# Moving the last weight's split, the opening fold and the fetches of rows in a two-layer graph network kernel

## The chip, the cores and the metric

The kernel runs on one core of a Trainium2 chip. The metric is the device time of one execution in microseconds (us); lower is better. Times shown are medians of several runs. A profile is one further execution under the hardware profiler; its times are those of that execution alone.

## The reference

A batch of 32 graphs, each with 512 nodes and 512 features, goes through two layers. Both share one 512 x 512 adjacency matrix of zeros and ones.

```python
def _L0_gnn_ref(x, adj, Wq, bq, Wk, bk, Wv, bv):        # 8 heads of 64
    q = (x @ Wq + bq).reshape(b, n, H, HD)
    k = (x @ Wk + bk).reshape(b, n, H, HD)
    v = (x @ Wv + bv).reshape(b, n, H, HD)
    scores = jnp.einsum('bihd,bjhd->bhij', q, k) / jnp.sqrt(jnp.float32(HD))
    mask = jnp.where(adj == 0, jnp.float32(-1000000000.0), jnp.float32(0.0))
    weights = jax.nn.softmax(scores + mask[None, None, :, :], axis=-1)
    return jnp.einsum('bhij,bjhd->bihd', weights, v).reshape(b, n, H * HD)

def _L1_gnn_ref(x, adj, weight, bias):
    y = jnp.einsum('nm,bmd->bnd', adj, x)
    return jnp.einsum('bnd,do->bno', y, weight) + bias

x = _layernorm(x + _L0_gnn_ref(x, adj, ...), axis=-1)
x = _layernorm(x + _L1_gnn_ref(x, adj, ...), axis=-1)
```

## The kernel before, in words

All work on one graph ("batch" b) fits on the chip. A product that needs full float32 precision is made from three passes over numbers split in two: HIGH (a rounded part), REST (the remainder) and BOTH (a correction). ScalarE makes HIGH, VectorE or GpSimd makes REST and BOTH. The passes accumulate in PSUM banks, of which there are eight, handed out in a ring by `bank` (L200). A bank can be written again only once its reader has emptied it.

The order of the work is written out by hand. Each engine runs its instructions in the order in which the Python code issues them, and SyncE (SP) issues nearly all transfers, in order too: a transfer that must wait holds back those behind it. Python lists of small steps are interleaved by `merge` (L786): unit k, then the steps of slot k behind it. `run` (L719) issues them.

`iteration(b)` (L796) is one round of the loop, for b = 0 to 30; `last_halves` and the code behind it finish the last graph. A round works on several graphs at once, a software pipeline:

- `attend(b, hp)` (L619) multiplies the exponentials of head pair hp by the values, into one bank; `turn_out` (L629) has VectorE transpose that bank (L637) into `attT` and SP write it to memory (`turned`, L639). `fetch_rows` (L641) reads it back with four transfers in row order (L645).
- `take_scores(b, 1)` makes the scores of the second four heads on TensorE (L602). VectorE adds the mask and empties the banks into `e` (L604), ScalarE takes exponentials (L606), GpSimd adds them over the key blocks into `es` (L617). There are two score stages in a round: the second half of batch b and, later, the first half of batch b + 1.
- `projections(b + 1)` makes queries and keys in eight units of 12 matmuls each (L417): q0, k0, q1, k1 in the first half of the round, the other four in the second. A unit's weight, split in three, is a `chunk` of 768 KB that is streamed from memory for every batch: `fetch_chunk` (L406, its transfer is L412) writes into a ring of three buffers, and `project` (L431) fetches chunk n + 3 right behind its matmuls, into the buffer that these just left. ScalarE (L428) and VectorE (L429) add bias and parts. In the first half only chunk k1 is fetched and used within the half; q2, k2 and q3 are used in the second half.
- `fold_squares` (L647) sums exponentials on VectorE (transposes L655, sums L657), `pass_parts` and `fetch_parts` (L661, L666) send these sums through memory to turn them, `add_up` (L673) inverts them (L677, L678). `scale_rows` (ScalarE, L691) and `add_rows` (GpSimd, L695) make the residual.
- `values` are 48 matmuls; `aggregate` and `convolve` are the second layer of batch b - 1. `turns` and `splits_of_x` prepare batch b + 2: VectorE transposes (L347), ScalarE makes HIGH (L304), VectorE REST (L307), GpSimd BOTH (L310). `AFTER` (L868) holds steps that a round leaves for the next one, run after the first head pair of attention (`sooner`) and after the scores (`later`).
- In rounds 2 to 5, `load_adjacency_rows` (L288) loads 128 rows of the adjacency (256 KB), and `look_for_low_half` (L292) looks whether rounding would lose something of them.

Before the loop, the opening (L900 to L952) makes batch 0's projections and values, splits the weights, and keeps the chunks in memory for the later batches. The weight of the second layer, `w1`, is loaded by `load_last_weight` (L747, transfers L750) in four pieces while batch 0's values are made. `split_last_weight` (L755) then does three activations (L757, L758, L760) and two GpSimd subtractions (L761, L762) for each piece, just before the loop. `w1` is first used by `convolve` at the end of round 1.

Tiles come from rings of buffers by tag. `xs` has two, and holds in turn the last chunk of the opening, the adjacency, and then the batches' rows, loaded by `load(b)` (L215). `turn` has six and serves many short-lived tiles.

Of the kernel before, what the change touches and what calls it, by code (L numbers as in the profile page):

```python
# [8 lines left out]
FP = mybir.dt.float32  # L9
FR = mybir.dt.float32r  # L10
I32 = mybir.dt.int32
U8 = mybir.dt.uint8
AF = mybir.ActivationFunctionType
# [5 lines left out]
P = 128  # L19
# [4 lines left out]
EPSILON = 2.0 ** -12  # L24
SHRINK = 1.0 - 2.0 ** -13
SQ = 32
TURNS = 6
# [151 lines left out]
HIGH, REST, BOTH = 0, 1, 2  # L179
# [3 lines left out]
def fast_kernel(ctx: ExitStack, tc, verdict, x, adj, Wq, bq, Wk, bk, Wv, bv, W1, b1, out):  # L183
    nc = tc.nc
    B, N, D = x.shape
    H = Wq.shape[1] // HD
    HP = H // 2
    NB = N // P
    DB = D // P
# [4 lines left out]
    work = ctx.enter_context(tc.tile_pool(name="work", bufs=2))  # L194
# [5 lines left out]
    def bank(*shape):  # L200

        return psum.tile([P, *shape], FP, name="bank", tag="bank", bufs=8)

    def plain(t):

        return t.bitcast(FP)
# [3 lines left out]
    def rows_tile(b):  # L210
        if b == B - 1:
            return work.tile([P, NB, D], FP, name="xlast", tag="wv", bufs=1)
        return work.tile([P, NB, D], FP, name="xs", bufs=2)

    def load(b):  # L215
        X[b] = rows_tile(b)
        nc.sync.dma_start(X[b], x[b].rearrange("(c p) d -> p c d", p=P))
# [16 lines left out]
    RAW = {}  # L234
# [53 lines left out]
    def load_adjacency_rows(c):  # L288
        IN["adj", c] = work.tile([P, N], FP, name="adj_rows", tag="turn", bufs=TURNS)
        nc.sync.dma_start(IN["adj", c], adj[c * P:(c + 1) * P, :])  # L290
# [10 lines left out]
    PAIRS = GROUP // 2  # L301
# [60 lines left out]
    def turns(b):  # L362
        return [(turn_squares, b, d) for d in range(DB)] if b < B else []

    def splits_of_x(b):
        return [[(f, b, d) for d in range(DB)] if b < B else [] for f in (high_of_x, rest_of_x, both_of_x)]
# [95 lines left out]
    def projections(b):  # L462

        return [(project, b, which, m) for which, m in SEQUENCE] if b < B else []
# [120 lines left out]
    def aggregation(b):  # L585

        return [[(f, b, d) for d in range(DB)] if b >= 0 else [] for f in (split, aggregate)]
# [31 lines left out]
    def attend(b, hp):  # L619
        po = bank(N)  # L620
        for j in range(NB):
            e = E.pop((b, hp, j))
            for s in range(2):
                h = 2 * hp + s
                nc.tensor.matmul(po[s * HD:(s + 1) * HD, :], V[b, j][:, h * HD:(h + 1) * HD], e[:, s, :],  # L625
                                 start=(j == 0), stop=(j == NB - 1))
        OUT[b, hp] = po

    def turn_out(b, hp):  # L629

        po = OUT.pop((b, hp))
        at = AT[b, hp] = work.tile([P, N], FP, name="attT")
        if b == B - 1:
            nc.scalar.activation(at, po, AF.Copy)
            return

        nc.vector.transpose(at, po)  # L637
        TURNED[b, hp] = passing.tile([P, N], FP, name="turned")
        nc.sync.dma_start(TURNED[b, hp], at)  # L639

    def fetch_rows(b, hp):  # L641
        rows = ROWS[b, hp] = work.tile([P, NB, P], FP, name="rows")
        turned = TURNED.pop((b, hp)).rearrange("(i r) (c j f) -> j r c i f", r=SQ, c=NB, f=SQ)
        for j in range(P // SQ):
            nc.sync.dma_start(rows[j * SQ:(j + 1) * SQ, :, :].rearrange("p c (i f) -> p c i f", f=SQ), turned[j])  # L645
# [73 lines left out]
    def run(units):  # L719
        for unit in units:  # L720
            unit[0](*unit[1:])
# [23 lines left out]
    both_of_chunk(1)  # L745

    def load_last_weight():  # L747
        for d in range(DB):
            RAW["w1", d] = work.tile([P, D], FP, name="raw", tag="qk"[d % 2] + "0", bufs=PAIRS)
            nc.sync.dma_start(RAW["w1", d], W1[d * P:(d + 1) * P, :])  # L750

    def values_weight(d):
        return RAW["v", d // 2][:, d % 2, :]

    def split_last_weight(d):  # L755
        w = RAW.pop(("w1", d))
        nc.scalar.activation(w, w, AF.Copy, scale=1.0 / EPSILON)  # L757
        nc.scalar.activation(w1[:, HIGH, d, :], w, AF.Copy, scale=SHRINK)  # L758
        temp = work.tile([P, N], FR, name="temp", tag="turn", bufs=TURNS)
        nc.scalar.activation(temp, w, AF.Copy, scale=EPSILON * SHRINK)  # L760
        nc.gpsimd.tensor_sub(w1[:, REST, d, :], w, plain(w1[:, HIGH, d, :]))  # L761
        nc.gpsimd.tensor_sub(w1[:, BOTH, d, :], plain(w1[:, REST, d, :]), plain(temp))  # L762

    def norm(t, which):

# [6 lines left out]
    def folds(b, g):  # L772
        return [(fold_squares, b, hp) for hp in range(g * PAIRS, (g + 1) * PAIRS)]
# [5 lines left out]
    def residuals(b, g):  # L779

        return [[(f, b, hp) for hp in range(g * PAIRS, (g + 1) * PAIRS)] for f in (scale_rows, add_rows)]
# [4 lines left out]
    def merge(units, behind):  # L786

        merged = []
        for k in range(max(len(units), len(behind))):
            merged += units[k:k + 1] + (behind[k] if k < len(behind) else [])  # L790
        return merged
# [4 lines left out]
    def iteration(b):  # L796

        units = projections(b + 1)
        scaled, added = residuals(b, 0)
        later_scaled, later_added = residuals(b, 1)  # L800
        turned, divided = turns(b + 2), splits_of_x(b + 2)
        splits, gathered = aggregation(b - 1)
        squares = [(load_squares, b + 2, d) for d in range(DB)]
        folded = folds(b, 1)

        attend(b, 0)
        turn_out(b, 0)
        sooner, later = AFTER.pop(b - 1, ([], []))
        run(sooner)
        attend(b, 1)  # L810
        turn_out(b, 1)
        if b > 0:
            fetch_parts(b, 0)
        take_scores(b, 1)
        run(later)
        fetch_rows(b, 0)
        fetch_rows(b, 1)
        look = []
        if 2 <= b < 2 + NB:
            load_adjacency_rows(b - 2)  # L820
            look = [(look_for_low_half, b - 2)]
        if b == 0:
            run(merge(units[:4], [[(fold_squares, b, 1), (pass_parts, b, 0), (fetch_parts, b, 0)], [], [(add_up, b, 0)],
                                  folded[:1]]))
        else:
            old, young = norm(b - 1, 1), norm(b - 1, 0)
            roots = slice(0, 2 * NB if b > 1 else NB)
            if b == 1:
                run(survey(0, 0))
            run(merge(units[:4], [[(square_root, b - 1, roots), (add_up, b, 0), (invert_root, b - 1, roots)],  # L830
                                  folded[:1] + old[2:], [(store, b - 2)] if b > 1 else [], young[2:] + scaled]))
        attend(b, 2)
        turn_out(b, 2)
        load(b)
        attend(b, 3)
        turn_out(b, 3)
        if b == 0:
            run(scaled)
        later = scores(b + 1, 0)
        run(added + later + folded[1:])  # L840

        run(merge(units[4:], [[(pass_parts, b, 1), (fetch_parts, b, 1)], look, [(fold_squares, b + 1, 0)], splits[:2]]))
        units = values(b + 1)
        chunks = [(fetch_chunk, (b + 2) * len(SEQUENCE) + n) for n in range(AHEAD)]
        squares += [(fetch_rows, b, 2), (fetch_rows, b, 3), (pass_parts, b + 1, 0)] + chunks
        run(merge(units, [[(add_up, b, 1)], [(fold_squares, b + 1, 1)] + squares, later_scaled if b == B - 2 else [],
                          turned[:1] + (later_added if b == B - 2 else [])]))
        if b == B - 2:
            load(B - 1)
        run(merge(gathered, [[unit] for unit in turned[1:]]))  # L850
        fresh, seen, shift = survey(b, 0), survey(b - 1), biases(b - 1)
        high, rest, both = divided
        if b == 0:
            run(high + rest + both[::-1] + later_scaled + later_added)
            return
        convolve(b - 1, FIRST_TWO)
        if b == B - 2:
            run([(add_row, b - 1, 0), (add_row, b - 1, 1)] + shift[:2] + fresh + seen[:2])
            return
        run(later_scaled + later_added[:1] + [(add_row, b - 1, 0)] + shift[:1] + later_added[1:])  # L860
        run([(add_row, b - 1, 1)] + shift[1:2] + seen[:1])
        convolve(b - 1, whole(2))
        run([(add_row, b - 1, 2)] + shift[2:3] + fresh[:1])
        convolve(b - 1, whole(3))
        run(high + rest + [(add_row, b - 1, 3)] + shift[3:] + both)
        AFTER[b] = (fresh[1:] + seen[1:2], seen[2:])

    AFTER = {}  # L868
# [74 lines left out]
    w1 = work.tile([P, 3, DB, N], FR, name="w1", bufs=1)  # L943
# [2 lines left out]
    load_last_weight()  # L946
    run(merge(values(0), [[unit] for unit in turns(1)]))
    high, rest, both = splits_of_x(1)
    run(high + rest + both[::-1])

    fold_squares(0, 0)
    run([(split_last_weight, d) for d in range(DB)])  # L952
    for b in range(B - 1):
        iteration(b)
    last_halves(B - 1)
# [63 lines left out]
```

## Time and profile before

| what | value |
|---|---|
| median of 3 runs | 2574.64 us (2574.56 to 2575.02) |
| the profiled execution's own time | 2578.16 us |
| its span, from the first to the last instruction | 2575.9 us |
| mean granted clock of TensorE | 0.999 |
| transfers | 380.47 MB, mean 148 GB/s |
| busy: TensorE, VectorE, GpSimd, ScalarE | 99%, 80%, 68%, 59% |

How to read the profile: PE is TensorE, DVE VectorE, ACT ScalarE, POOL GpSimd, SP the queue that issues transfers. L417 is line 417 of the kernel before. A timeline line gives start, duration (us), engine, line, operation, what is written from what, how many instructions, and in brackets how long the engine was idle before and what ended the wait. A window line gives the stretch, its length, then for each engine the busy time and the number of instructions, the clock, the share of time that the DMA engines were busy and GB/s. Consecutive instructions of one kind are merged in a timeline, so pauses inside a merged line do not show. A matmul's end is modelled; lengths of TensorE's stages are read as differences of starts. Every landing of a transfer that the text gives is from the trace.

### The profile page before, as it was taken

The page shows a single profiled execution, that of the slowest core. Times are in us where ns is not written, and L with a number is a line of the kernel's source. Part 1 is how long each engine was busy: PE and PEld are TensorE (multiplying, and loading weights), DVE is VectorE, ACT ScalarE, POOL GpSimd, SP SyncE. Part 2 cuts the span into 40 slices and gives each one's busy share as a digit, 9 for nine tenths or more (in the row PEclk, how much of TensorE's full clock was granted, in tenths as well). Part 3 has the DMA queues.
Part 4 walks back from the last instruction along what each step waited for, and adds up shares of the span by engine and source line. Part 5 has one row for each costly group of instructions (what it writes and reads, how often), then busy time and mean ns, then how long its engine had stood idle before and what let it go on. Part 6 is the DMA issues. An engine that isn't in the chain of part 4 may idle for free.

```text
span 2575.9 us, 35702 instructions
## 1 busy us (share of the span) xinstructions
PE 2562.7 (99%) x11324; PEld 1693.9 (66%) x11324; DVE 2058.9 (80%) x3795; ACT 1527.3 (59%) x2540; POOL 1751.0 (68%) x1105
## 2 busy tenths in 40 slices
PE   9999999999999999999999999999999999999998
PEld 6566666766667666666667666676766667666666
DVE  8778788787787887878878778887788787887878
ACT  5666655657556665556665566655656556565555
POOL 5766676666766666766667667676766766666767
PEclk9999999999999999999999999999999999999999
DMA  9655554655545545456454464454654545545431
GB/s 267 165 158 142 159 146 125 174 140 162 148 112 167 152 151 162 110 154 176 135 160 119 143 178 136 153 138 129 172 141 161 143 117 167 145 157 164 103 124 52
DMA packets 675042, 380.47 MB, mean 148 GB/s; under 512 B 586912, under 2 KB 591264, under 8 KB 674848
## 3 DMA queue, kind: packets, MB, share of 16 engines
q1 hardware_dynamic: 674416, 377.48, 51.3%
q8 instruction: 92, 1.51, 0.2%
q14 instruction: 102, 0.84, 0.1%
q10 hardware_dynamic: 432, 0.66, 0.1%
HBM read 303.57 MB, written 74.45 MB: 147 GB/s over the span
## 4 chain that ended last, share of the span: by engine, by line
PE 94%; DVE 2%; DMA 1%; POOL 1%; ACT 1%; issue 0%; SPq 0%; DVEq 0%; ACTq 0%; POOLq 0%
PE bank L417 52%; PE bank L602 17%; PE bank L625 16%; PE bank L526 9%; DVE e L604 1%; DMA stream<-kept_k 0%; DMA turned<-attT 0%; DVE bnst L477 0%; DVE factors L307 0%; POOL es L617 0%; ACT e L606 0%; SPq L645 0%; POOL factors L310 0%; PE bank L729 0%; POOL wv L932 0%
## 5 line engine op out<-in xcount | busy, mean ns | idle before, releaser
L417 PE MATMUL bank<-factors,stream 128*128 128x512 f32 x3012 | 704.3, 392 | 2.9 <-DMA stream<-kept_k 2.3
L606 ACT ACTIVATE e<-e 128x1024 f32<-128x1024 f32 x512 | 525.3, 1055 | 300.7 <-DVE e L604 262.3
L417 PEld LDWEIGHTS bank<-factors,stream 128*128 128x128 f32 x3012 | 560.1, 188 | 167.7 <-DVE e L604 23.5
L617 POOL TENSOR_TENSOR es<-es,e 128x1024 f32<-128x1024 f32 x256 | 615.9, 2406 | 20.1
L604 DVE SCALAR_TENSOR_TENSOR e<-gap,bank 128x512 f32<-128x512 uint8 x1024 | 617.6, 678 | 12.1 <-PE bank L602 12.1
L617 POOL TENSOR_TENSOR es<-e 128x1024 f32<-128x1024 f32 x128 | 305.8, 2389 | 425.6 <-ACT e L606 425.6
L602 PE MATMUL bank<-q,k 64*128 64x512 f32 x2048 | 464.9, 598 | 0.7 <-DVE attT L637 0.7
L625 PE MATMUL bank<-e,v 128*64 128x512 f32 x2048 | 453.6, 595 | 0.0
L602 PEld LDWEIGHTS bank<-q,k 64*128 64x128 f32 x2048 | 204.1, 186 | 259.9 <-issue 157.3
L417 PE MATMUL bank<-w,factors 128*128 128x512 f32 x1536 | 354.4, 389 | 0.5 <-POOL factors L310 0.5
L417 PE MATMUL bank<-wv,factors 128*128 128x512 f32 x1536 | 353.5, 389 | 0.0
L310 POOL TENSOR_TENSOR factors<-factors,factors 128x512 fp32r<-128x512 f32 x255 | 322.1, 1284 | 33.9 <-DVE factors L307 32.0
L691 ACT ACTIVATE rows<-rows,zero,inverse 128x64 f32<-128x64 f32 x992 | 335.0, 429 | 9.7 <-DVE inverse L678 9.7
L417 PEld LDWEIGHTS bank<-w,factors 128*128 128x128 f32 x1536 | 288.0, 188 | 61.3 <-POOL factors L310 1.3
L417 PEld LDWEIGHTS bank<-wv,factors 128*128 128x128 f32 x1536 | 288.2, 188 | 60.6 <-DVE e L604 0.8
L625 PEld LDWEIGHTS bank<-e,v 128*64 128x64 f32 x2048 | 141.4, 137 | 278.4 <-issue 265.4
L503 ACT ACTIVATE high<-xs 128x512 fp32r<-128x512 f32 x124 | 74.4, 627 | 333.3 <-PE bank L526 333.2
L504 POOL TENSOR_TENSOR low<-xs,high 128x512 fp32r<-128x512 f32 x124 | 159.2, 1295 | 156.3 <-PE bank L526 156.3
L541 POOL TENSOR_TENSOR xs<-xs,b_r 128x512 f32<-128x512 f32 x124 | 159.8, 1289 | 125.3 <-DVE xs L561 125.3
L637 DVE STREAM_TRANSPOSE attT<-bank 128x512 f32<-128x512 f32 x124 | 87.6, 708 | 159.1 <-PE bank L625 159.1
L493 ACT ACTIVATE xs<-xs,shift,rstd 128x512 f32<-128x512 f32 x248 | 181.5, 805 | 14.7 <-DVE shift L488 14.7
L695 POOL TENSOR_TENSOR xs<-xs,rows 128x512 f32<-128x512 f32 x124 | 160.6, 1306 | 22.6 <-ACT rows L691 14.9
(98 smaller groups left out, 2433.4 us busy)
## 6 DMA issues: line engine op xcount, KB each, us to landing
stream<-kept_q SPq DMA_DIRECT2D x124, 768.0 KB, 5.9
stream<-kept_k SPq DMA_DIRECT2D x124, 768.0 KB, 4.3
xin<-in_x_dram SPq DMA_DIRECT2D x496, 64.0 KB, 2.3
turned<-attT SPq DMA_DIRECT2D x124, 256.0 KB, 3.2
rows<-turned SPq DMA_DIRECT2D x496, 64.0 KB, 2.4
xs<-in_x_dram SPq DMA_DIRECT2D x31, 1024.0 KB, 6.1
out_dram<-xs SPq DMA_DIRECT2D x31, 1024.0 KB, 5.1
part<-passed SPq DMA_DIRECT2D x256, 8.0 KB, 1.7
```

The lines of the kernel that those rows point to most:

```text
L310: engine.tensor_sub(both, plain(high), plain(rest))
L417: nc.tensor.matmul(pm, left(f, d), right(f, d), start=(f != REST and d == 0), stop=(f != HIGH and d == DB - 1))
L493: nc.scalar.activation(row, row, AF.Identity, bias=SHIFT[t][:, slot:slot + 1], scale=RSTD[t][:, slot:slot + 1])
L526: nc.tensor.matmul(pm, part, adjT[:, n % NB, :], start=(n == 0), stop=(n == 2 * NB - 1))
L541: nc.gpsimd.tensor_add(X[b][:, c, :], X[b][:, c, :], b1_r)
L602: nc.tensor.matmul(ps[s], keys[:, j * P:(j + 1) * P], queries, start=True, stop=True)
L604: nc.vector.scalar_tensor_tensor(e[:, s, :], gap[:, j, :], NEG * root, ps[s], op0=ALU.mult, op1=ALU.add)
L606: nc.scalar.activation(e, e, AF.Exp, scale=1.0 / root)
L617: nc.gpsimd.tensor_add(ES[b, hp], ES[b, hp] if j > 1 else E[b, hp, 0], E[b, hp, j])
L625: nc.tensor.matmul(po[s * HD:(s + 1) * HD, :], V[b, j][:, h * HD:(h + 1) * HD], e[:, s, :], start=(j == 0), stop=(j == NB - 1))
L691: nc.scalar.activation(part, part, AF.Identity, bias=zero, scale=inverse[:, c, s:s + 1])
L695: nc.gpsimd.tensor_add(cols, cols, ROWS.pop((b, hp)))
```

## The change

The change has three parts.

1. The last weight is loaded by one transfer into a tile of the `xs` ring. Its split moves out of the opening into round 0, behind the values of batch 1. It runs in two passes: first HIGH and REST of all four pieces, then ScalarE writes HIGH times EPSILON over the raw weight, and GpSimd subtracts this from REST. It has still twelve activations and eight subtractions; the four temporary tiles are gone.
2. In the opening, the remainders (REST) and corrections (BOTH) of batch 1's input are no longer issued ahead of `fold_squares(0, 0)` but left in `AFTER[-1]`, so that round 0 issues them after the first head pair's `attend` and `turn_out`.
3. In round 1, both `fetch_rows`, and in rounds 2 to 5 the second one, move from ahead of the projections to behind the first unit, that is, behind the fetch of chunk k1. In rounds 2 to 5 the adjacency rows are loaded behind `load(b)` instead of ahead of the projections. Round 0 and rounds from 6 on keep their order.

```diff
--- before.py
+++ after.py
@@ -745,21 +745,21 @@
     both_of_chunk(1)
 
     def load_last_weight():
-        for d in range(DB):
-            RAW["w1", d] = work.tile([P, D], FP, name="raw", tag="qk"[d % 2] + "0", bufs=PAIRS)
-            nc.sync.dma_start(RAW["w1", d], W1[d * P:(d + 1) * P, :])
+        RAW["w1"] = work.tile([P, DB, D], FP, name="xs", bufs=2)
+        nc.sync.dma_start(RAW["w1"], W1.rearrange("(c p) f -> p c f", p=P))
 
     def values_weight(d):
         return RAW["v", d // 2][:, d % 2, :]
 
-    def split_last_weight(d):
-        w = RAW.pop(("w1", d))
-        nc.scalar.activation(w, w, AF.Copy, scale=1.0 / EPSILON)
-        nc.scalar.activation(w1[:, HIGH, d, :], w, AF.Copy, scale=SHRINK)
-        temp = work.tile([P, N], FR, name="temp", tag="turn", bufs=TURNS)
-        nc.scalar.activation(temp, w, AF.Copy, scale=EPSILON * SHRINK)
-        nc.gpsimd.tensor_sub(w1[:, REST, d, :], w, plain(w1[:, HIGH, d, :]))
-        nc.gpsimd.tensor_sub(w1[:, BOTH, d, :], plain(w1[:, REST, d, :]), plain(temp))
+    def split_last_weight():
+        w = RAW["w1"]
+        for d in range(DB):
+            nc.scalar.activation(w[:, d, :], w[:, d, :], AF.Copy, scale=1.0 / EPSILON)
+            nc.scalar.activation(w1[:, HIGH, d, :], w[:, d, :], AF.Copy, scale=SHRINK)
+            nc.gpsimd.tensor_sub(w1[:, REST, d, :], w[:, d, :], plain(w1[:, HIGH, d, :]))
+        for d in range(DB):
+            nc.scalar.activation(w[:, d, :], plain(w1[:, HIGH, d, :]), AF.Copy, scale=EPSILON)
+            nc.gpsimd.tensor_sub(w1[:, BOTH, d, :], plain(w1[:, REST, d, :]), w[:, d, :])
 
     def norm(t, which):
 
@@ -813,12 +813,11 @@
             fetch_parts(b, 0)
         take_scores(b, 1)
         run(later)
-        fetch_rows(b, 0)
-        fetch_rows(b, 1)
-        look = []
-        if 2 <= b < 2 + NB:
-            load_adjacency_rows(b - 2)
-            look = [(look_for_low_half, b - 2)]
+        waiting = [(fetch_rows, b, 0), (fetch_rows, b, 1)]
+        looking = 2 <= b < 2 + NB
+        look = [(look_for_low_half, b - 2)] if looking else []
+        ready = 1 if looking else 0 if b == 1 else 2
+        run(waiting[:ready])
         if b == 0:
             run(merge(units[:4], [[(fold_squares, b, 1), (pass_parts, b, 0), (fetch_parts, b, 0)], [], [(add_up, b, 0)],
                                   folded[:1]]))
@@ -827,11 +826,14 @@
             roots = slice(0, 2 * NB if b > 1 else NB)
             if b == 1:
                 run(survey(0, 0))
-            run(merge(units[:4], [[(square_root, b - 1, roots), (add_up, b, 0), (invert_root, b - 1, roots)],
+            run(merge(units[:4], [waiting[ready:]
+                                  + [(square_root, b - 1, roots), (add_up, b, 0), (invert_root, b - 1, roots)],
                                   folded[:1] + old[2:], [(store, b - 2)] if b > 1 else [], young[2:] + scaled]))
         attend(b, 2)
         turn_out(b, 2)
         load(b)
+        if looking:
+            load_adjacency_rows(b - 2)
         attend(b, 3)
         turn_out(b, 3)
         if b == 0:
@@ -847,6 +849,8 @@
                           turned[:1] + (later_added if b == B - 2 else [])]))
         if b == B - 2:
             load(B - 1)
+        if b == 0:
+            split_last_weight()
         run(merge(gathered, [[unit] for unit in turned[1:]]))
         fresh, seen, shift = survey(b, 0), survey(b - 1), biases(b - 1)
         high, rest, both = divided
@@ -946,10 +950,9 @@
     load_last_weight()
     run(merge(values(0), [[unit] for unit in turns(1)]))
     high, rest, both = splits_of_x(1)
-    run(high + rest + both[::-1])
-
+    run(high)
     fold_squares(0, 0)
-    run([(split_last_weight, d) for d in range(DB)])
+    AFTER[-1] = (rest + both[::-1], [])
     for b in range(B - 1):
         iteration(b)
     last_halves(B - 1)
```

## The prediction, made before the change was run

> **What bounds the kernel now.** I read the page's busy times first. TensorE is busy for 99% of the span, so the ceiling on a change that leaves the matmuls alone is what TensorE loses to waits.
>
> ```profile
> PE 2562.7 (99%) x11324; PEld 1693.9 (66%) x11324; DVE 2058.9 (80%) x3795; ACT 1527.3 (59%) x2540; POOL 1751.0 (68%) x1105
> ```
>
> The busy share hides slow pacing, so next I cut the trace into one window per loop round. Each begins where a batch's first attention matmul begins (rounds 1 to 6, of which 2 to 5 carry the adjacency look).
>
> ```profile
> 115.17:196.74 81.57, 79.87 (x354) 52.55 (x353) 63.63 (x114) 51.63 (x95) 55.55 (x35) 1.00 0.58 165
> 196.74:276.62 79.88, 79.85 (x353) 52.53 (x353) 64.82 (x120) 47.86 (x82) 54.81 (x34) 1.00 0.53 150
> 276.62:357.07 80.45, 79.81 (x353) 52.54 (x352) 64.83 (x121) 47.88 (x82) 54.80 (x34) 1.00 0.53 149
> 357.07:436.69 79.62, 79.62 (x354) 52.62 (x353) 64.83 (x120) 47.88 (x82) 54.81 (x34) 1.00 0.52 151
> 436.69:517.05 80.36, 79.86 (x355) 52.54 (x354) 65.03 (x121) 47.88 (x82) 54.81 (x34) 1.00 0.53 149
> 517.05:596.66 79.61, 79.61 (x354) 52.62 (x354) 63.50 (x118) 47.34 (x81) 54.34 (x34) 1.00 0.51 148
> ```
>
> The second column is the length. An undisturbed round takes 79.61 us (the last one); rounds 1, 2, 3 and 5 are longer by 1.96, 0.27, 0.84 and 0.75 us. From here on the kernel repeats. So I read TensorE's timeline, first an undisturbed round (517 us on), then rounds 0 and 1.
>
> ```profile
> 524.06 7.21 PE L602 MATMUL bank<-q,k 64*128 64x512 f32 x32
> 531.20 11.21 PE L417 MATMUL bank<-factors,stream 128*128 128x512 f32 x48
> 542.34 7.09 PE L625 MATMUL bank<-e,v 128*64 128x512 f32 x32
> ```
>
> Differences of starts give stage lengths: scores (L602) 531.20 - 524.06 = 7.14 us, first half of the projections (L417) 542.34 - 531.20 = 11.14.
>
> ```profile
> 56.91 8.27 PE L602 MATMUL bank<-q,k 64*128 64x512 f32 x32
> 65.11 11.17 PE L417 MATMUL bank<-factors,stream 128*128 128x512 f32 x48
> ...
> 83.23 2.85 PE L602 MATMUL bank<-q,k 64*128 64x512 f32 x12
> 86.74 6.48 PE L602 MATMUL bank<-q,k 64*128 64x512 f32 x20 [0.66 <-DVE attT L637]
> 93.15 11.22 PE L417 MATMUL bank<-factors,stream 128*128 128x512 f32 x48
> ...
> 129.33 8.49 PE L417 MATMUL bank<-factors,stream 128*128 128x512 f32 x36
> 139.52 2.97 PE L417 MATMUL bank<-factors,stream 128*128 128x512 f32 x12 [1.70 <-DMA stream<-kept_k]
> ```
>
> Round 0's two score stages take 65.11 - 56.91 = 8.20 and 93.15 - 83.23 = 9.92 us, 1.06 and 2.78 over the reference. Only 0.66 of these 3.84 us shows as idle: the rest is TensorE pacing itself on banks that VectorE empties late. Round 1's projection half waits 1.70 us for a k chunk, the fourth of the half. Why VectorE is late in round 0 stands in the timelines of ScalarE and VectorE:
>
> ```profile
> 59.85 0.63 ACT L757 ACTIVATE raw<-raw 128x512 f32<-128x512 f32 x1 [7.88 <-DMA raw<-in_L_gnn_weight_dram]
> 66.68 7.68 ACT L606 ACTIVATE e<-e 128x1024 f32<-128x1024 f32 x8
> 74.27 0.66 ACT L428 ACTIVATE q<-bank,bq_c 128x512 f32<-128x512 f32 x1
> ```
> ```profile
> 74.96 0.69 DVE L429 TENSOR_TENSOR q<-bank,q 128x512 f32<-128x512 f32 x1 [6.17 <-ACT q L428]
> 82.60 0.27 DVE L677 TENSOR_REDUCE inverse<-part 128x16 f32<-128x64 f32 x1 [3.38 <-DMA part<-passed]
> ```
>
> ScalarE stands 7.88 us before the last weight, splits it until 66.78, and only then takes the exponentials; VectorE idles 6.17 us for the bias add behind them, then 3.38 us for the sums' round trip, and reaches the transposes of the attention output (L637) at 85.98, after TensorE wants their banks. And the late chunk of round 1, in the SP queue:
>
> ```profile
> 129.07 5.32 SPq L645 DMA_DIRECT2D rows<-turned  x8
> 134.48 0.57 SPq L412 DMA_DIRECT2D stream<-kept_k  x1
> ```
>
> The chunk's buffer is free about 129.33 + 2.75 = 132.1 (a quarter of the half), but eight row fetches stand ahead of it until 134.39.
>
> **What the Trainium skill says.** "DMA: Bandwidth & Descriptors", section "Anatomy of one DMA": a semaphore wait happens on the issuing sequencer, not in the DMA engines. The trace agrees: the chunk issues 0.09 us after the last row fetch. The same page, "Queues, rings and completion order": each DMA engine consumes one queue's descriptors in ring order. The trace agrees: the first head's turned tile, issued at 58.67, lands at 62.51, 0.68 after the last of the four weight loads (61.83). "SBUF — State Buffer", "Who interferes with whom": a VectorE operation with two SBUF inputs is blocked while GpSimd holds the shared port. The trace agrees: the first remainder (L307, 0.68 us otherwise) at 51.24 takes 2.60 us, over GpSimd's L617 that ends at 53.29.
>
> **Fold ahead of remainders (round 0's opening).** Now VectorE does four remainders (51.24 to 55.65), four fold operations (55.57 to 58.02), two L637 transposes, and starts the mask-and-add L604 at 59.18, 2.27 us after the scores start; in round 1 it is 123.35 - 122.19 = 1.16 us. Afterwards the fold runs at 51.24 to 53.7, the first L637 to 54.3 (its bank is ready near 49.90 + 3.70 = 53.6, the delay of the same step at 142.42), the remainders to 54.3 + 4 x 0.61 = 56.7 without GpSimd in the way, the second L637 at 56.91 + 0.13 = 57.04. L604 then starts at 58.07: **-1.06 us** on the path. GpSimd's four L310 (4.96 us) follow the remainders, 56.7 to 61.7; they are needed 1.84 us into the first projection, at 65.9. Cover lost, the wait would be what exceeds 4.2 us.
>
> **Last weight out of round 0's start.** Twelve activations and eight subtractions leave ScalarE and GpSimd between 59.85 and 71.73. Exponentials start near 59.5 and end near 68.9, the bias add comes 4.7 us after the projections start (as at 134.06 against 129.33), so near 69.6 instead of 74.96. Fold of head pair 1 to 72.5, its sums' round trip 4.55 us (78.05 to 82.60 now): add-up at 77.2, third fold near 78.4 to 80.8 (its GpSimd sums are ready by 69), L637 at 80.8 and at 82.9. TensorE then wants the first bank six banks, 2.85 us, into the stage. Slack: 1.4 us on VectorE. So the second stage is 7.14 too: **-2.78 us**. With VectorE's slack gone, each further us of round trip costs up to one, at most the 2.78 again.
>
> **Where the split goes.** Twelve activations x 0.62 = 7.4 us into an idle stretch of ScalarE (12.50 us ahead of 116.68) and eight GpSimd subtractions x 1.31 (pitch at 61.22 to 71.73) = 10.5 us into one of 12.29 us ahead of 120.89: cost **0**. ScalarE's second pass waits for GpSimd's remainders, some 6 us after its own start, still 2 us before the next splits. GpSimd's last subtractions can hold VectorE's first remainder for up to 0.9 us; the second L637 waits for TensorE anyway, with 0.94 us to spare. Uncovered, 0 to 0.6 us. The weight is first used near 185, far off. One load of 1 MB instead of four of 256 KB moves the same bytes: 0. It lies in an xs buffer that the next load needs only at 147.
>
> **A new wait in round 0.** Its rows still go ahead of the chunk (the order changes from round 1 on). Their start hangs on the turned tile behind the weight (62.51), not on VectorE, so the fourth chunk still lands at 72.64, the trace's landing now. TensorE wants it at 64.05 + 8.3 = 72.35 instead of 73.4: about 0.3 us, with the restart 0.5. Bounds 0 (landing 0.4 earlier) and 0.9. I take **+0.5**.
>
> **Rows behind the chunk, round 1.** The chunk issues near 132.4 and takes 3.8 to 4.9 us (undisturbed 3.97 at 534.28; 4.90 here), so lands by 137.3, needed at 137.6: 13.09 (142.42 - 129.33) becomes 11.14, **-1.95**. The eight rows issue 5.3 us long behind it and land near 140.5; ScalarE scales them at 145.03, so 4.5 us of cover.
>
> **Half of the rows and the adjacency rows behind the chunk, rounds 2 to 5.** SP is on time there (the chunk issues 3.05 to 3.09 after the half begins), but 64 KB rows and a 256 KB load lie ahead in the ring and landing takes 5.3, 5.9, 4.6 and 5.8 us; about 5.2 is allowed. Taking four rows and about 0.7 us of adjacency data out gives 4.3 to 4.9: **-(0.27 + 0.84 + 0 + 0.75) = -1.86**. The adjacency rows, now behind the batch load, land near 316 in round 3; the look uses them at 322.83. The later two-row fetches have the same cover as in round 1.
>
> **Sum.** -1.06 - 2.78 + 0.5 - 1.95 - 1.86 = -7.15 us. The profiled execution took 2578.16 us, span 2575.9; its span should become 2568.8. The median shown, 2574.64, lies 3.5 under that execution's time; waits are differences within the program, so I take the sum off it: **2567.5 us** (-0.28%).
>
> **Rivals.** (a) The sums' round trip takes the place of the weight: it comes earlier but behind other queue entries, and the second score stage stays long. VectorE's 3.38 us idle speaks for it, 1.4 us slack against. 2567.5 + 2.8 = 2570.3. (b) The chunks stay late since the DMA engines, not the order, are slow: landings of 5.9 us in round 3 against 4.6 in round 4 with the same queue speak for it. Rounds 1 to 5 keep 3.8 us: 2571.3. (c) The split is moved but nothing gained, because opening waits only shift: 2574.6. (d) **Slower**: row fetches behind the chunk land after ScalarE wants to scale; the exponentials of the next batch queue behind that, and TensorE with them, in rounds 1 to 5. Cover is 4.5 us; every us beyond costs 5 us in all. It decides once rows land 4.5 + 7.15 / 5 = 5.9 us later than reckoned; at 7 us, 2567.5 + 12.5 = 2580. Row landings of 2 to 3 us after issue speak against it.
>
> **How the numbers follow.** Forecast 0.66 (own range 2566.2 to 2569.2), (a) 0.13, (b) 0.12, (c) 0.04, (d) 0.05. What a measurement can tell from no change is about 0.2%, 5.15 us: faster is below 2569.5, so the forecast and a part of (a), 0.71; within, the rest of (a), (b), (c), 0.24; slower, (d), 0.05. The range, 2566.2 to 2571.5, takes in (a) and (b), the k chunk's bounds and 0.5 us more for the opening.
>
> **What would show it.** Right: both score stages of round 0 at 7.14, rounds 1 to 5 at 79.6, ScalarE's exponentials near 59.5, the split in the gap ahead of 113, a small wait for the fourth chunk of round 0. Wrong: L637 still the releaser in round 0, chunk waits in rounds 1 to 5, or new waits on GpSimd's L310 or on the scaled rows.

## The result, and the profile after

The changed kernel took 2569.23 us (median of 16 runs, 2568.46 to 2571.19), the kernel before beside it 2574.43 us (16 runs). The ratio is 0.998, 95% interval 0.9973 to 0.9987: 5.2 us faster, at the edge of the 0.2% named above. That is 0.03 us outside the forecast's own range (2566.2 to 2569.2) and inside the wider one, which takes in rivals (a) and (b). The profiled execution of the changed kernel took 2569.64 us, its span is 2567.9 us. A second set of runs of the same kernel gave a ratio of 0.9978 (0.9969 to 0.9987).

TensorE's share of busy time on the page has hardly anywhere left to go:

```profile
PE 2557.3 (100%) x11324; PEld 1692.1 (66%) x11324; DVE 2058.6 (80%) x3795; ACT 1528.6 (60%) x2540; POOL 1751.1 (68%) x1105
```

The windows of rounds 1 to 6, cut as before (stretch, length, busy time and count for TensorE, weight loads, VectorE, ScalarE, GpSimd, then clock, share of DMA, GB/s):

```profile
112.00:192.34 80.34, 79.82 (x353) 52.56 (x352) 63.82 (x114) 51.51 (x95) 58.99 (x38) 1.00 0.61 167
192.34:271.89 79.55, 79.55 (x354) 52.64 (x353) 64.81 (x120) 47.87 (x82) 54.81 (x34) 1.00 0.53 151
271.89:351.44 79.55, 79.55 (x354) 52.64 (x353) 64.82 (x120) 47.86 (x82) 54.83 (x34) 1.00 0.53 151
351.44:431.24 79.80, 79.80 (x354) 52.55 (x353) 64.81 (x119) 47.87 (x82) 54.84 (x34) 1.00 0.54 150
431.24:510.77 79.53, 79.53 (x354) 52.63 (x353) 65.05 (x121) 47.88 (x82) 54.86 (x34) 1.00 0.54 151
510.77:590.30 79.53, 79.53 (x353) 52.63 (x352) 63.52 (x118) 47.34 (x81) 54.35 (x34) 1.00 0.53 148
```

An undisturbed round is 79.53 us here and was 79.61 in the profile of before. No step of the change explains that: the same code runs at 79.53 in some sets of runs and at 79.60 in others, and the medians of the kernel before follow (2574.4 and 2574.3 with the one, 2576.7 and 2577.0 with the other). So a span is never compared below across sets; each round is measured against the undisturbed one of its own trace. By that, round 1 still loses 0.81 us and round 4 0.27. The two spans differ by 8.0 us, of which this change of pace is over 2.

TensorE's timeline of rounds 0 and 1:

```profile
57.19 7.21 PE L602 MATMUL bank<-q,k 64*128 64x512 f32 x32
64.33 8.45 PE L417 MATMUL bank<-factors,stream 128*128 128x512 f32 x36
72.93 3.00 PE L417 MATMUL bank<-factors,stream 128*128 128x512 f32 x12 [0.15 <-DVE part L657]
75.86 7.09 PE L625 MATMUL bank<-e,v 128*64 128x512 f32 x32
82.88 7.21 PE L602 MATMUL bank<-q,k 64*128 64x512 f32 x32
90.02 11.18 PE L417 MATMUL bank<-factors,stream 128*128 128x512 f32 x48
...
126.16 8.45 PE L417 MATMUL bank<-factors,stream 128*128 128x512 f32 x36
135.14 3.00 PE L417 MATMUL bank<-factors,stream 128*128 128x512 f32 x12 [0.52 <-DMA stream<-kept_k]
```

Both score stages of round 0 are 7.14 us (64.33 - 57.19 and 90.02 - 82.88), from 8.20 and 9.92. The fourth unit of the first projection half begins at 72.93 instead of 72.62 (64.33 + 8.29), the small new wait that was forecast; the half is 0.4 us longer than an undisturbed one (11.53 against 11.10). The line names VectorE, but chunk k1 landed at 72.80 and VectorE had nothing that this unit needs: it is the DMA. Round 1 still waits for its chunk. ScalarE and VectorE in round 0:

```profile
59.73 4.64 ACT L606 ACTIVATE e<-e 128x1024 f32<-128x1024 f32 x4 [7.47 <-DVE e L604]
64.82 4.33 ACT L606 ACTIVATE e<-e 128x1024 f32<-128x1024 f32 x4 [0.45 <-POOL es L617]
69.06 0.67 ACT L428 ACTIVATE q<-bank,bq_c 128x512 f32<-128x512 f32 x1
```
```profile
54.51 2.46 DVE L307 SCALAR_TENSOR_TENSOR factors<-factors,turn 128x512 fp32r<-128x512 f32 x4
...
69.77 0.69 DVE L429 TENSOR_TENSOR q<-bank,q 128x512 f32<-128x512 f32 x1 [1.76 <-ACT q L428]
...
79.16 0.26 DVE L677 TENSOR_REDUCE inverse<-part 128x16 f32<-128x64 f32 x1 [5.13 <-DMA part<-passed]
...
82.53 1.30 DVE L637 STREAM_TRANSPOSE attT<-bank 128x512 f32<-128x512 f32 x2
```

The exponentials start at 59.73 instead of 66.68, and the bias add no longer waits 6 us. The four remainders take 2.46 us instead of 4.41, since GpSimd no longer holds the first one up. The sums' round trip is now what VectorE waits for (5.13 us), and the transposes L637 end only 0.2 us before the masks need VectorE. The split's new place, on GpSimd:

```profile
105.39 5.07 POOL L759 TENSOR_TENSOR w<-xs,w 128x512 fp32r<-128x512 f32 x4
110.43 5.01 POOL L762 TENSOR_TENSOR w<-w,xs 128x512 fp32r<-128x512 f32 x4
117.94 4.97 POOL L310 TENSOR_TENSOR factors<-factors,factors 128x512 fp32r<-128x512 f32 x4 [2.50 <-DVE factors L307]
```

Its eight subtractions end at 115.44, 2.5 us before GpSimd's next work. They cost nothing on the path. The SP queue of round 1:

```profile
129.20 0.34 SPq L412 DMA_DIRECT2D stream<-kept_k  x1
129.65 6.56 SPq L645 DMA_DIRECT2D rows<-turned  x8
```

The chunk is issued 3.04 us into the half, as early as it can be, with nothing ahead of it. It landed 5.80 us later all the same (135.00).

### The profile page after: what moved, and what is told of

Read it like the earlier page. It is cut to its first block, busy times and chain, and to the rows that moved or that the text cites. A ratio compares the mean times of both kernels' runs of the same rounds, so it can differ in the third digit from the quotient of the medians.

```text
span 2567.9 us, 35669 instructions
## 1 busy us (share of the span) xinstructions
PE 2557.3 (100%) x11324; PEld 1692.1 (66%) x11324; DVE 2058.6 (80%) x3795; ACT 1528.6 (60%) x2540; POOL 1751.1 (68%) x1105
## 4 chain that ended last, share of the span: by engine, by line
PE 98%; DVE 1%; DMA 0%; issue 0%; POOL 0%; ACT 0%; DVEq 0%; ACTq 0%
PE bank L417 54%; PE bank L602 18%; PE bank L625 17%; PE bank L526 9%; DVE e L604 0%; DMA stream<-kept_k 0%; DVE bnst L477 0%; POOL factors L310 0%; DMA xin<-in_x_dram 0%; DVE early L316 0%; DVE factors L307 0%; DVE xlast L561 0%; DVE xs L557 0%; DVE xlast L557 0%; PE bank L701 0%
## 5 line engine op out<-in xcount | busy, mean ns | idle before, releaser
L310 POOL TENSOR_TENSOR factors<-factors,factors 128x512 fp32r<-128x512 f32 x255 | 321.9, 1282 | 25.4 <-DVE factors L307 24.7
L637 DVE STREAM_TRANSPOSE attT<-bank 128x512 f32<-128x512 f32 x124 | 87.8, 709 | 156.4 <-PE bank L625 156.4
```

The lines of the kernel that those rows point to most:

```text
L310: engine.tensor_sub(both, plain(high), plain(rest))
```

## The experiments

My theory after the result: the round 0 terms are right; in rounds 1 to 5 the saving was overestimated, since the first profile drew unusually late chunks and since rows behind a chunk hinder it too. The rival: order in the queue decides alone, as the forecast had it, and round 1's wait is an accident. In what follows, "excess" is a round's length over the undisturbed round of the same trace (79.60 us, a mean, in both profiles of the kernel before), and a landing is the time from the issue of chunk k1 to its landing.

**The kernel before, again.** No edit.

> The kernel before, unchanged, profiled once more. If the waits in its first profile are fixed by the program: rounds 1, 2, 3 and 5 are again 1.95, 0.27, 0.84 and 0.75 us over 79.6, and the score stages of round 0 take 8.20 and 9.92 us. If the chunk's landing is a matter of chance from one execution to the next, as the profiled execution's 2578.2 us against a median of 2574.4 suggests: round 0 as before, but another set of rounds late, by about 1 to 2 us in all instead of 3.8. Timed against itself: ratio 1.000.

Ratio 1.000 (0.9992 to 1.0009). In the new profile rounds 1 to 5 have an excess of 1.39, 0.32, 0.01, 0.69 and 0.01 us, 2.42 in all against 3.87 (1.97, 0.28, 0.85, 0.02, 0.75) in the first; round 0's second score stage is 8.95 against 9.92. Which rounds wait, and how long, changes from one execution to the next. So a sum of waits from one trace is one draw.

**Parts 1 and 2 alone; part 3 alone.** In the first kernel, the fetches of rows and adjacency are back where they were:

```diff
-        run(waiting[:ready])
+        fetch_rows(b, 0)
+        fetch_rows(b, 1)
+        if looking:
+            load_adjacency_rows(b - 2)
```

> The weight's split moved and the fold ahead, but rows and adjacency where they were. By the forecast's sum: -1.06 - 2.78 + 0.5 = -3.3 us against before, both score stages of round 0 at 7.14, rounds 1 to 5 as late as in before. If the chunk's lateness in the timed runs is worth only about 1.5 us, this kernel is nearly as fast as the changed one (within 1.5 us); if it is worth the 3.8 us of the first profile, it is 3.8 us slower than the changed one.

Ratio 0.9988 (0.9981 to 0.9995): -2.96 us (2573.76 against 2576.72). Round 0 goes to 61.75 us; the second score stage is 7.45, not 7.14. The second kernel is the kernel before with the third part of the change only.

> Only rows and adjacency moved behind the chunks; opening and split as before. By the forecast -3.8 us against before. If the first profile of before drew unusually late chunks, -1 to -2 us. Round 0 as before (8.20 and 9.92 us). If rows behind the chunk slow its landing, round 1 still waits some 0.5 us or more for chunk k1, landing near 5.8 us.

Ratio 0.9991 (0.9983 to 0.9999): -2.05 us. The interval reaches from -0.3 to -4.4 us, so the time alone doesn't exclude the forecast's -3.8; the profiles below tell more. Round 1's chunk lands after 5.62 us, rounds 1 to 5 have an excess of 1.26 in all. The two gains add up to 5.0 us, the whole change's 5.2: in this cut the parts are independent, as far as intervals of about 2 us either way can tell.

**Rows behind the chunk in every round.**

```diff
-        ready = 1 if looking else 0 if b == 1 else 2
+        ready = 0 if b > 0 else 2
```

> The changed kernel with both row fetches behind chunk k1 in every round from 1 on. If only what lies ahead of the chunk in the queue delays it (the forecast's reckoning): chunk landings of 4.0 to 4.5 us in all rounds and no change against the changed kernel. If rows that follow right behind it slow it: landings of 5.2 to 5.8 us in every round as in round 1 of the changed kernel, each round 0.3 to 0.8 us longer, 30 rounds, so 10 to 20 us slower than the changed kernel.

Ratio 0.9999 (0.999 to 1.0007): the whole gain is lost again. In rounds 6 to 29 the median landing is 5.00 us against 4.23 in the changed kernel, where rows go ahead; six of 24 landings exceed 5.2 us, none does there. Rounds 1 to 30 have an excess of 6.4 us. Round 10, in TensorE's timeline and in the SP queue of this kernel:

```profile
845.12 8.50 PE L417 MATMUL bank<-factors,stream 128*128 128x512 f32 x36
853.88 3.00 PE L417 MATMUL bank<-factors,stream 128*128 128x512 f32 x12 [0.27 <-DMA stream<-kept_k]
```
```profile
848.21 0.34 SPq L412 DMA_DIRECT2D stream<-kept_k  x1
848.65 6.29 SPq L645 DMA_DIRECT2D rows<-turned  x8
855.04 0.65 SPq L412 DMA_DIRECT2D stream<-kept_q  x1
```

The chunk landed 5.54 us after its issue, at 853.75. Not all of the excess is of this kind: 1.4 us of it stand in the second halves of rounds 5 and 27, where chunk k3 is late (6.0 and 5.4 us after its issue) with no rows behind it. There the transfers that stand behind the rows in the queue were later too, and the last of them landed 1.6 to 1.8 us after k3 was issued.

The loss is smaller than the 10 to 20 us expected, since most landings stay just within the 5.2 us allowed. But the direction is plain: rows that follow a chunk delay its landing. That the queue ran empty before the chunk is not the reason: chunk k3, issued 5 us after the last landing and followed by nothing for 3 us, lands in 4.19 us (median, rounds 6 to 28 of the changed kernel).

The trace's records of single DMA packets narrow the delay down. With rows behind it, the last of the chunk's 128 packets ends 4.01 us after the issue; for chunk k3 in the changed kernel it is 3.81 (medians of rounds 6 to 28). But the landing, the signal that TensorE waits for, comes 1.04 us after that last packet, against 0.39. So most of the delay is not in moving the chunk's data. It lies between the last packet and the signal, while the rows' packets of 128 bytes are under way (the first of them begins 3.4 us after the chunk's issue).

**Only the adjacency moved in rounds 2 to 5.**

```diff
-        ready = 1 if looking else 0 if b == 1 else 2
+        ready = 0 if b == 1 else 2
```

> The changed kernel, but in rounds 2 to 5 both row fetches go ahead of the chunk again; only the adjacency rows stay moved. If rows ahead of the chunk delay it (forecast): landings of about 4.8 us in rounds 2 to 5 or more, no gain or a loss up to 0.5 us against the changed kernel. If rows behind it slow it and the adjacency alone was the hindrance: landings of 4.0 to 4.5 us in rounds 2 to 5 as in later rounds, those rounds at 79.55, up to 0.5 us faster than the changed kernel.

Ratio 0.9977 (0.9968 to 0.9987). Landings in rounds 2 to 5 are 4.20, 4.75, 4.49 and 4.33 us, none of those rounds has an excess over 0.02. So the adjacency alone was the hindrance there, and the change's move of the second row fetch isn't needed. In time the kernel isn't told apart from the changed one (0.998 and 0.9978).

**Rows of round 1 behind the second unit.** In addition to the edit above, both fetches of round 1 stand behind chunk q2, and the second one of round 0 behind chunk k1.

```diff
-        ready = 0 if b == 1 else 2
+        ready = (1, 0)[b] if b < 2 else 2
...
-            [waiting[ready:] + [(square_root, ...), ...], folded[:1] + old[2:], ...
+            [[(square_root, ...), ...], waiting[ready:] + folded[:1] + old[2:], ...
```

> As the kernel with only the adjacency moved, and in round 1 both row fetches go behind the second unit's chunk fetch instead of the first's, in round 0 the second row fetch goes behind chunk k1. If rows right behind a chunk slow it: round 1's chunk lands in about 4.3 us instead of 5.8 and its wait of 0.5 us (0.8 us of stage length) goes; round 0's half is shorter by up to 0.4 us, unless rows slow that chunk as well. In all 0.8 to 1.5 us faster than the changed kernel. If they do not: round 1's chunk still lands after 5 us or more, no difference.

Ratio 0.9976 (0.9967 to 0.9986), no difference from the last kernel, so the gain that was expected did not come. Round 1's chunk lands in 4.38 us and the round is 79.61, but in the last kernel, with the rows right behind it, it landed in 5.03 us, which is also in time. Over eight executions with the rows right behind, round 1's landing was 4.70 to 5.80 us, late in two. Round 0 is 61.86 against 61.85.

**Part 1 alone.** The weight's split moved, the remainders ahead of the fold, rows and adjacency as before:

```diff
-    run(high)
+    run(high + rest + both[::-1])
     fold_squares(0, 0)
-    AFTER[-1] = (rest + both[::-1], [])
```

> The weight's split alone is moved, remainders stay ahead of the fold, rows and adjacency as before. By the forecast: first score stage of round 0 stays at 8.2, the second goes to 7.14: -2.78 us against before, less up to 0.5 for chunk k1. If the second stage needs the fold's earlier start as well, it stays above 7.14 and the gain is smaller.

Ratio 0.999 (0.9982 to 0.9999): -2.35 us. The score stages of round 0 are 8.18 and 7.40: as forecast, each stage has its own cause, though the second stays 0.26 us above 7.14.

**Part 2 alone.** The fold ahead of the remainders in the kernel before, with the split where it was:

```diff
-    run(high + rest + both[::-1])
+    run(high)
     fold_squares(0, 0)
+    AFTER[-1] = (rest + both[::-1], [])
     run([(split_last_weight, d) for d in range(DB)])
```

> The fold alone goes ahead of the remainders; the split stays in the opening. By the forecast: first score stage of round 0 at 7.14 (-1.06 us), the second stays near 9.9 since ScalarE still stands before the last weight: -1.06 us against before. A rival: the second stage grows by what the first one gains, as its late VectorE steps hang on the weight's landing and not on the scores, and nothing is gained.

Both expectations fell: ratio 1.004 (1.0026 to 1.0053), 9.1 us **slower**. TensorE's and GpSimd's timelines of this kernel:

```profile
57.28 7.21 PE L602 MATMUL bank<-q,k 64*128 64x512 f32 x32
64.42 2.14 PE L417 MATMUL bank<-factors,stream 128*128 128x512 f32 x8
76.20 11.93 PE L417 MATMUL bank<-factors,stream 128*128 128x512 f32 x40 [9.65 <-POOL factors L310]
```
```profile
60.86 1.28 POOL L761 TENSOR_TENSOR w<-raw,w 128x512 fp32r<-128x512 f32 x1 [7.22 <-DMA turned<-attT]
...
69.99 1.27 POOL L762 TENSOR_TENSOR w<-w,temp 128x512 fp32r<-128x512 f32 x1
71.22 4.94 POOL L310 TENSOR_TENSOR factors<-factors,factors 128x512 fp32r<-128x512 f32 x4
```

The first score stage is 7.14, as expected. But the corrections L310 moved along with the remainders, and on GpSimd they now stand behind the split's eight subtractions, which wait for the weight. They end at 76.16; the first projection wants them 1.9 us into its run. Without the first part, the second is a loss.

**The changed kernel, again.**

> The changed kernel, unchanged, on the same chip and beside the same runs of before as the three kernels that follow. If its profile is typical: rounds 2 to 5 with chunk landings of 4.7 to 5.3 us, round 1 between 4.8 and 5.8 us, 5 us faster than before (ratio 0.998), and up to 1 us slower than the kernel that moves only the adjacency in rounds 2 to 5. If round 1's wait in its first profile was chance, round 1 is near 79.6 here.

Ratio 0.9978 (0.9969 to 0.9987). Rounds 1 to 5 have an excess of 0.39 us in all, 0.30 of it in round 5 (landing 5.26); round 1 is in time (4.95 us). Round 0 is 61.52, its second score stage 7.25.

**Fold earlier in round 0**, on the kernel with only the adjacency moved:

```diff
         if b == 0:
+            fold_squares(b, 1)
-            run(merge(units[:4], [[(fold_squares, b, 1), (pass_parts, b, 0), ...
+            run(merge(units[:4], [[(pass_parts, b, 0), ...
```

> The kernel with only the adjacency moved in rounds 2 to 5, and in round 0 the fold of head pair 1 ahead of the first projection unit's bias add, in an idle stretch of VectorE (1.8 us). If the round trip of the sums now limits round 0's second score stage (7.55 us in that kernel, 7.14 undisturbed), it starts up to 1.8 us earlier and the stage goes to 7.14: 0.4 us less, round 0 at 61.45 instead of 61.85. If it is the fold behind the round trip, or the wait only moves to the fourth chunk, round 0 stays at 61.85.

Inconclusive: ratio 0.9979 (0.9971 to 0.9987). The second stage is 7.14, but in this execution chunk k1 came 1 us late (12.34 us for the half), which gives VectorE time anyway. Whether the earlier fold helps stays open.

**Adjacency load in rounds 2 to 29, ahead of the chunk and behind the batch's load.** Both kernels start from the one with only the adjacency moved, and repeat load and look in every round:

```diff
-        looking = 2 <= b < 2 + NB
+        looking = 2 <= b < B - 2
```

The first puts the load ahead of the units, the second leaves it behind `load(b)`.

> Load and look of adjacency rows in each of rounds 2 to 29 (they are repeated; the output is the same), the load ahead of chunk k1 where the kernel before had it, both row fetches ahead too. If 256 KB ahead of the chunk in the queue delay it (forecast): chunk landings of 4.6 to 5.9 us in every round and rounds 0.2 to 0.8 us longer, 8 to 20 us in all against the next kernel. If the late landings of rounds 2 to 5 came from elsewhere: landings of 4.0 to 4.5 us, no difference from the next kernel.

> The same load and look in each of rounds 2 to 29, but the load behind the batch's load, as the change puts it. Both theories: chunk landings of 4.0 to 4.5 us, rounds of 79.6, within 1 us of the kernel that moves only the adjacency in rounds 2 to 5. If the load there disturbs later transfers (batch load, chunk k3), rounds are longer by that.

Ahead: ratio 1.0004 (0.9995 to 1.0012), 2575.53 us. Behind: 0.9979 (0.997 to 0.9988), 2569.0 us. The 6.5 us between them are the price of 28 loads in the wrong place, less than the 8 to 20 us expected. The SP queue of round 12 with the load ahead, where the chunk landed 4.50 us after its issue:

```profile
998.86 5.32 SPq L645 DMA_DIRECT2D rows<-turned  x8
1004.22 0.62 SPq L290 DMA_DIRECT2D adj_rows<-in_adj_dram  x1
1005.51 0.34 SPq L412 DMA_DIRECT2D stream<-kept_k  x1
```

Landings in rounds 6 to 29:

| what stands around chunk k1 in the queue | kernel | median landing | least to most |
|---|---|---|---|
| rows ahead | changed | 4.23 us | 4.02 to 4.95 |
| rows ahead, adjacency load elsewhere in every round | loads behind | 4.16 us | 3.89 to 4.74 |
| rows and adjacency load ahead | loads ahead | 4.86 us | 4.25 to 5.63 |
| nothing ahead, rows right behind | rows behind | 5.00 us | 4.49 to 5.75 |

The second kernel's excess in rounds 2 to 29 is 0.3 us in all: the load does no harm where the change puts it.

## Why the prediction was right, and which term was too large

**First score stage of round 0, -1.06.** Right: 8.20 to 7.14, for the reason given, with the start of the masks 1.16 us after the stage's start. But the step hid a condition. "Cover lost, the wait would be what exceeds 4.2 us" named the price of late corrections, and no step asked what stood ahead of them on GpSimd. With the weight's split still there, it was 9.65 us.

**Second score stage, -2.78.** Nearly right: 9.92 to 7.14 in the first profile after, to between 7.14 and 7.55 in the others. The slack of 1.4 us was mis-sized. It took the sums' round trip at 4.55 us; it is 6.3 (the fold's end at 72.83 to L677 at 79.16). The first of its two transfers, L664, lands after 3.2 us instead of 1.5, though chunk k1 had landed just before it was issued; why is open. Rival (a), the round trip as the next limit, is true at 0 to 0.4 us, not 2.8.

**The split's new place, 0.** Right: the gap of GpSimd held it with 2.5 us to spare. VectorE's first remainder there took 0.87 us, 0.2 longer than the others, and nobody waited.

**The new wait in round 0, +0.5.** Right in mechanism and size (0.4 us), wider in range: the weight landed at 61.65, the turned tile at 62.36, the rows kept the queue until 67.86, and the chunk landed at 72.80. In other executions of kernels with these two parts it cost between 0 and 1.5 us; the bound of 0.9 was too tight. The longest, in the kernel with the adjacency load behind in every round, which does the same work in round 0:

```profile
63.53 8.48 PE L417 MATMUL bank<-factors,stream 128*128 128x512 f32 x36
73.23 3.01 PE L417 MATMUL bank<-factors,stream 128*128 128x512 f32 x12 [1.23 <-DVE q L429]
```
```profile
62.47 5.43 SPq L645 DMA_DIRECT2D rows<-turned  x8
68.00 0.57 SPq L412 DMA_DIRECT2D stream<-kept_k  x1
```

TensorE reached the projections early (63.53), the weight landed no earlier than in the other runs (61.76), and the chunk landed at 73.10.

Together, round 0 went from 65.27, 64.34 and 65.72 us (three profiles with the old opening, mean 65.1) to between 61.5 and 63.0 (eight profiles with both parts, leaving out the earlier fold, mean 61.9): -3.2 us, against a forecast of -3.34.

**Rounds 1 to 5, -3.81.** This is the mis-sized term. The timed part 3 alone gave -2.05 us, with a wide interval. The profiles agree with that: with the old order of the queue (the kernel before twice, parts 1 and 2, part 1 alone, part 2 alone), the excess of rounds 1 to 5 is 3.87, 2.42, 3.00, 3.10 and 1.99 us, mean 2.9; with the change's order (three profiles) it is 1.12, 1.26 and 0.39, mean 0.9. So 1.0 us of the error is that the first profile was an unlucky draw, and 0.9 us is that the waits don't all go. The step that failed is "taking four rows and about 0.7 us of adjacency data out gives 4.3 to 4.9", with its like in round 1, "takes 3.8 to 4.9 us". The adjacency half of it holds (4.86 to 4.16 us). The rows half is reversed: rows ahead of the chunk cost it nothing when SP is early enough, rows right behind it cost 0.8 (5.00 against 4.23 us). In rounds 2 to 5 the change removed one hindrance and added another; landings went from about 5.1 to 4.8 (medians of four rounds range from 4.6 to 5.5 in the five profiles with the old order, and are 4.7, 4.8 and 5.2 with the new one). In round 1, where rows ahead hold the queue for 2 us, moving them back is still right.

**The sum.** -3.2 - 2.0 = -5.2 us, against -7.15. That this meets the measured gain to a tenth is luck, since the waits of single profiles scatter by more. The forecast, 2567.5, was 1.7 us too low, and the measured time is inside the stated range since that range left room for (a) and (b). The median shown was 2574.64, and taking waits of a trace off the median of the runs assumed that the trace is a typical run. Its own time, 3.5 us above that median, spoke against it. Part of the 3.5 is a slower pace (79.60 against 79.53 us in a round), part more waits.

**The rivals.** (b) did not hold as a whole, since the order in the queue mattered (4.86 against 4.16 us); that landings vary from one execution to the next, which it stood on, explains 1.0 us of the missing 1.9. (c) and (d) did not happen: in round 1 the rows were scaled from 140.66, after they landed at 139.04, with 1.6 us to spare rather than 4.5. Of the missing 2.9, 1.7 is that the rows landed later in the half than reckoned. The other 1.2 is that the start of the scaling (145.03) was read in a round that was itself 1.95 us late.

## What to carry to other kernels

Where a program waits only now and then, profile it more than once before waits are added up, and measure each against the undisturbed round of the same trace. When a step is moved past another, ask on every engine that works for it what it now stands behind: the same three lines of this change shorten a stage by 1 us with the weight's split out of the way (8.18 to 7.14) and cost 9 us with it. A transfer that is needed soon should be issued with neither large data ahead of it nor many small packets right behind it.

## What the runs showed that was not expected

Transfers that follow one in the same queue can delay its landing: eight row fetches (64 KB each) issued from 0.45 us behind a 768 KB chunk raise its median landing from 4.2 to 5.0 us over 24 rounds, as much as 256 KB ahead of it (4.86). Issue order on SP alone doesn't tell when data land. Most of this delay stands between the end of the chunk's last packet and the signal of its landing, 1.04 us instead of 0.39. What holds the signal back was not shown; that the rows' small packets do is the nearest guess.
